# A scan layer, two FFNs and a higher-order linear attention in one kernel: front rounds, one q product, weight parts and a bias put in other places of a hand-written order

## The chip, the cores and the metric

The kernel runs as one program on one core of a Trainium2 chip. The metric is the device time of one execution in microseconds (us), as the median of several runs. One profiled execution beside them gives the trace from which all durations here are read.

## The reference

The input x has the shape (2, 2048, 256) in f32. Four layers are added to it one after the other, each on a layer norm of x:

```python
x = x + scan_layer(_layernorm(x))
x = x + ffn(_layernorm(x))
x = x + hla(_layernorm(x))
x = x + ffn(_layernorm(x))          # the same weights

# scan_layer: RMS norm with gamma, then
qkva = einsum('bnd,ed->bne', xn, w_qkva); q, kv, a = three parts; a = sigmoid(a)
s_t = a_t * s_(t-1) + kv_t;  out = q * s

# ffn: ternary weights w_t = clip(round(w / mean|w|), -1, 1)
out = gelu(x @ W1.T + b1) @ W2.T + b2                 # 256 -> 1024 -> 256

# hla: 16 heads of 64 dims; per head and time step
kC = k @ C;  G += k (x) kC;  S += k (x) k;  C += q (x) v
out = q @ (S @ C - G)                                 # then all heads @ W_o
```

## The kernel before, in words

x (4096 rows) stays in SBUF as `x_sb`, 32 chunks of 128 rows; a *block* is 4 chunks (512 rows, 8 blocks), a *pair* is the n-th chunk of both batches (16 pairs). The program has three stages in time: the front (0 to 227 us), attention (227 to 940 us, the last FFN's first two blocks woven into its end) and the rest of the last FFN. The order of the instructions on PE, DVE, ACT and POOL is the order in which the Python code issues them (`manual_schedule`); every engine works through its own list and waits, with semaphores, for what the others have to deliver, or for a buffer to come free. SP's queue carries most of the transfers.

**Front** (`front`, L563 to L746). The scan layer runs ahead of the FFN. The loop over `i` makes one *round* per block: `ffn_in` (L505) gives the 1024 hidden columns in 8 steps of 4 products (L512; PE) with a Gelu each (L518; ACT), and after two of them ACT casts the pair to a high part (L491) and DVE subtracts it for the low part (L497). `ffn_out` (L523) makes 4 x 16 output products with both parts (L536) and DVE adds them to x. The FFN's products run in fp32r, each operand x or h as hi plus lo, so the normed rows are cast and subtracted too, transposed. What a block needs ahead of its round is cut into steps: `fs_` (statistics on DVE L162 and L163, four small POOL operations L173 to L181), `fq_` (rows on ACT L194, then the squares of the transpose through DRAM: DVE, two kinds of SP transfers), and `fe_` (`halves_end`: the hi cast on ACT L202, the lo subtraction on DVE L203). `ffn_bias` (L550) adds b2 to a block: a copy of one column of `b2_sb` onto itself on DVE (L552), which ties the order, then 1024 columns on POOL (L554). Rounds 4 to 7 have no scan work; they take the later blocks' steps, the attention's first norm (the three functions in `then`: `attention_stats`, `attention_rows`, `attention_turned`) and, on POOL, the weight parts in `later`.

**Weight parts.** q, k and v of one pair are each made by seven products in place of eight (`class Seven`, Strassen-Winograd). They need sums of quarters of the weights: `weights_kv` (L465) makes four of 128x512 for each of wk, wv and wq with POOL instructions L469 to L472 (T3 overwrites a quarter of the weight itself). `pair_sums` (L768) makes the sums of the pair's rows (POOL L778, four of 128x128). wv is loaded ahead of the rounds, wq in round 5.

**Attention** (`attention`, L756 to L1216). 32 steps s = (n, b): pair n, batch b. A step computes the 64x64 head products (`products`, `inter`, `intra`: L887, L904, L918), the state updates (`update`), and the product with W_o (`outward`, L967). The matrices k and u are needed in two layouts; the transpose (*turn*) goes DVE L259 (32x32 squares), SP to DRAM and back, ACT L986. Between them stand the `Seven.go` calls of the next pair. `go(i)` makes product i and then its copy from PSUM on ACT (i = 1, 5, 6, 4; L847 to L864) or its addition on DVE (0, 7, 3; L838). PSUM is divided by tag: oT and uT each have two banks, ps four; a product into a bank waits until the last content is out. The loop's prologue (from L1008) makes pair 0's seven products of k, q and v, and the statistics, rows and turn of pair 1. In the last pairs `last` (class `Last`) does the same for the first block of the last FFN: its `part` method issues one transfer pair of a weight that comes back from DRAM (`weights(True)`: w1r over wk; `weights(False)`: w2r over wv), on ACT's queue. `last.begin` sets up the first block's `ffn_in`, and `fill(n)` runs n of its 8 steps between the steps of the last pair. Then the loop at L1370 does the last FFN over the 8 blocks: `ffn_out` of block i, `ffn_bias` of block i + 1.

A product may be split by columns: `in_two` and `first_in_two` list the products of k and v that are made as two of 256 columns in place of one of 512; the second list holds for pair 0 only.

The instructions themselves come to the engines by DMA: the page's queue "instruction" has 158 packets in 2.59 MB.

Of the kernel before, what the change touches and what calls it, by code (L numbers as in the profile page):

```python
# [23 lines left out]
P = 128  # L24
B, T, D = 2, 2048, 256
ND = D // P
# [18 lines left out]
def kernel(  # L45
# [456 lines left out]

        return Hidden(g0, room), lambda a: pool.tile([P, 2, BT], FP, tag="h", bufs=2, name=f"h{g0}_{a}")

    def ffn_in(g0, rhs, hid, stage_, tag="ps"):  # L505


        for f in range(NF):
            ph = bank([P, BT], f"h{g0}_{f}", tag)
            for d in range(ND):  # L510
                for k, r in enumerate(rhs):
                    nc.tensor.matmul(  # L512
                        ph, lhsT=w1r[:, d, f * P : (f + 1) * P], rhs=r[:, d, :],
                        start=(d == 0 and k == 0), stop=(d == ND - 1 and k == 1),
                    )
            if f % 2 == 0:
                h = stage_(f // 2)
            nc.scalar.activation(h[:, f % 2, :], ph, AF.Gelu, bias=b1_sb[:, f : f + 1])  # L518
            if f % 2 == 1:
                hid.split(h)  # L520
            yield
# [34 lines left out]
    def run(steps, n=None):  # L556
        for _ in steps if n is None else zip(range(n), steps):
            pass
# [4 lines left out]
    def front(scan_pool, ffn_pool, tern_pool, then, later):  # L563
# [112 lines left out]
        for i in range(NB):  # L676
            u, g0 = i + 5, blocks[i]
            more, scans = i + 1 < NB, u < len(units)
            hid, staged = hidden(ffn_pool, g0)
            steps = ffn_in(g0, fn.pop(i), hid, staged)  # L680
            if i == 0:
                ffn_bias(g0)
            if scans:
                ys[u] = []
                products = scan_steps(scan_pool, units[u][0], xnT[u], last[units[u][0] // CPB], ys[u], 2 if i > 0 else 1)
                for j in range(4):
                    run(products, 1)
                    run(steps, 1)
                    if i == 0 and j == 0:
                        a_(4)  # L690
                        fq_(1)
                run(products)
                if i == 3:
                    fq_(5, scan_pool, "xn")
            else:
                run(steps, 4)
                if i == 4:
                    fs_(7)
                if i == NB - 2:
                    then[0]()  # L700
            if u + 1 < len(units):
                s_(u + 1)
            if i == 0:
                fs_(2)
            run(steps)
            if u + 1 < len(units):
                r_(u + 1)
            if i == 5:
                wq = const.tile([P, ND, H * DK], FP, tag="wq", name="wq")
                nc.sync.dma_start(out=wq, in_=w_q.rearrange("(c p) e -> p c e", p=P))  # L710
            if not more:
                wo = const.tile([P, NPR, D], FP, tag="wo", name="wo")
                nc.sync.dma_start(out=wo, in_=w_o.rearrange("(c p) e -> p c e", p=P))
                then[2]()

            steps = ffn_out(g0, hid, tag="out")
            if i > 3 and i - 4 < len(later):
                later[i - 4]()
            if i == 2:
                ffn_weights_away()  # L720
            if scans:
                fe_(i + 1)
                ffn_bias(blocks[i + 1])
                run(steps, 2)
                a_(u)
                run(steps, 3)
                if u + 1 < len(units):
                    t_(u + 1)
            if i < 3:
                fq_(i + 2)  # L730
                fs_(i + 3)
                if i == 2:
                    fs_(6)
            elif i == 3:
                fq_(6)
                fe_(5)
            elif i + 2 < NB:
                fe_(i + 2)
                ffn_bias(blocks[i + 1])
                if i + 3 < NB:  # L740
                    fq_(i + 3)
            elif more:
                ffn_bias(blocks[i + 1])
            if i == NB - 2:
                then[1]()
            run(steps)  # L746


# [7 lines left out]
    def attention(keep, pool, state, last):  # L756
# [22 lines left out]
            pairs[n] = x, S  # L779

        in_two = {"kN": (1, 5, 3), "vN": (1, 5)}
        first_in_two = {"kN": (2, 4, 6, 7), "vN": (2, 4, 6)}

        class Seven:

# [29 lines left out]
            def product(self, at, i, tag=None):  # L815

                new = tag is not None
                shape = [P, NPR // 2, P] if self.nm == "qT" else [P, HK]
                if new:
                    setattr(self, at, bank(shape, f"h{self.nm}{self.n}_{at}", tag))  # L820
                to = getattr(self, at)
                if self.nm == "qT":
                    for j in range(NPR // 2):
                        nc.tensor.matmul(  # L824
                            to[:, j, :], lhsT=self.B[i][:, j * P : (j + 1) * P], rhs=self.A[i],
                            start=(new and j == 0), stop=True, skip_group_check=True,
                        )
                else:
                    m = 2 if i in in_two[self.nm] or self.n == 0 and i in first_in_two[self.nm] else 1
                    for j in range(m):  # L830
                        cols = slice(j * HK // m, (j + 1) * HK // m)
                        nc.tensor.matmul(  # L832
                            to[:, cols], lhsT=self.A[i], rhs=self.B[i][:, cols],
                            start=(new and j == 0), stop=True, skip_group_check=True,
                        )
# [170 lines left out]

        NS = len(steps)
        pair_sums(0)  # L1008
        stats = norm_stats(norm_pool, pair(1), bias=True)
        k, q, v = Seven(0, "kN", "oT"), Seven(0, "qT", "uT"), Seven(0, "vN", "oT")  # L1010
        k.go(2, 1, 0, 5)
# [21 lines left out]
        for s in range(NS):  # L1033
# [24 lines left out]
                k.go(2)  # L1058
            if first and s > 0:
                units_end(s - 1)  # L1060
            if s < NS - 2:
                last.part()
            elif s == NS - 2:
                last.part()
            if s >= 3:
                outward(s - 3, 1)
# [5 lines left out]
            if not more and not first:  # L1072
                units_end(s - 1)
            evict(s, "uT")
            if not more:
                if first:
                    units_out(s)
# [61 lines left out]
            if not more:  # L1139
                fill(1)  # L1140
                if first:
                    turn_end(s + 1, "kT")
                else:
                    last.his()
                    last.second_rows()
            elif first:
                k.go(*((6, 3, 7) if s > 0 else (3,)))
            else:
                v.go(7)
                q.go(7)  # L1150
                if s == NS - 3:
                    last.part()
                v.go(3, 4)
                q.go(3)
            last.part()
            if first and s > 0 and more:
                units_out(s)
# [5 lines left out]
            if not more:  # L1163
                if first:
                    fill(1)
                    last.his()
                last.los()
            elif first:
                k.go(4)
                if n + 2 < CPB:  # L1170
                    xn = norm_rows(norm_pool, pair(n + 2), stats)
                else:
                    last.rows()
            else:
                q.go(4)
            if not first and s + 2 < NS:
                keys_out(s + 2)
# [7 lines left out]
                last.turned()  # L1185
            if s == NS - 4:
                last.weights(True)
            last.part()
            if s == NS - 3:
                last.part(None)  # L1190
                last.weights(False)
# [22 lines left out]
        outward(NS - 1, 0)  # L1214
        outward(NS - 1, 1)
        last.halves(2)  # L1216

    pairs = {}

# [15 lines left out]
    class Last:  # L1235
# [69 lines left out]
        def begin(self, first):  # L1305
            if first:
                self.hid = Hidden(self.g0, self.halves_room)
                self.hid.held = []
                self.steps = ffn_in(self.g0, self.rhs, self.hid, self.staged)

        def fill(self, n):
            run(self.steps, n)
# [25 lines left out]
    with (  # L1338
        tc.tile_pool(name="scan", bufs=2) as scan_pool,
        tc.tile_pool(name="ffn1", bufs=2) as ffn_pool,  # L1340
        tc.tile_pool(name="tern", bufs=2) as tern_pool,
        tc.manual_schedule(engines=by_hand),
    ):

        warm = bank([P, P], "warm")
        for _ in range(12):
            nc.tensor.matmul(warm, lhsT=ones, rhs=ones, start=True, stop=True)
        nc.scalar.activation(table, ones[:, :1], AF.Sigmoid)
        front(
            scan_pool, ffn_pool, tern_pool, (attention_stats, attention_rows, attention_turned),  # L1350
            [lambda: weights_kv(wk, wk_t), lambda: weights_kv(wv, wv_t), lambda: weights_kv(wq, wq_t)],
        )
    front_ctx.close()

# [1 line left out]
    with tc.tile_pool(name="keep", bufs=3) as keep_pool:  # L1356
# [10 lines left out]
        with tc.tile_pool(name="ffn2", bufs=1) as ffn_pool, tc.manual_schedule(engines=by_hand):  # L1367
            two_rings()
            steps, rhs, raws = last.outs, last.turns, {}
            for i, g0 in enumerate(blocks):  # L1370
                more, ahead = i + 1 < len(blocks), i + 3 < len(blocks)
                if i > 0:
# [6 lines left out]
                    steps = ffn_out(g0, hid, True, "out")  # L1379
                    if i + 2 < len(blocks):  # L1380
                        rhs[i + 2] = halves_end(raws.pop(i + 2), rows_room(ffn_pool, blocks[i + 2], bufs=2))
                if more:
                    ffn_bias(blocks[i + 1])
                if ahead:
                    if i > 0:
# [40 lines left out]
```

## Time and profile before

| what | us |
|---|---|
| three runs: lowest, median, highest | 1054.04, 1056.1, 1056.45 |
| the profiled execution: its own time | 1052.7 |
| its span in the trace | 1050.9 |
| front: PE's first product of attention starts at | 227.09 |
| granted TensorE clock, mean over the span | 1.0 |

The page divides the span in 40 slices of 26.3 us; a digit is the busy share in tenths:

```
PE   9999999999999999999999999999999999999998
POOL 3433233831101001010010110101101001023430
PEclk9999999999999999999999999999999999999999
```

PE is busy in every slice, at full clock. POOL is used in the front, then little until the last FFN's biases. The share alone says nothing of a moment in which PE waits: those are found in the timeline, as the distance between the start of a group of products and the start of the next, against the usual distance. A line of the timeline reads: start in us, length in us (from the first to the last of a run of equal instructions), engine, line of the code, operation, out<-in, shape, count; a bracket at its end gives the idle time of the engine just before and what ended it. "issue" in a bracket is time in which no semaphore held the engine.

### The profile page before, as it was taken

Reading aid. Unit: us, or ns where it says so; the run is one execution under the profiler, and the core shown is the slowest. Engines: PE = TensorE matmul, PEld = TensorE weight load, DVE = VectorE, ACT = ScalarE, POOL = GpSimd, SP = SyncE. Lnnn points to the kernel's source line nnn. Section 1 sums busy time; section 2 is a strip of 40 time slices with the busy share of each in tenths; the row PEclk is TensorE's granted clock in tenths of the full one; section 3 lists DMA queues with packets and bytes.
Section 4 is the critical chain, followed back from the end, with each engine's and each line's share of the span. In section 5 each row is a group of like instructions: output and inputs, shape, how many; then the busy total and the mean of one; then the engine's idle time right before and its main releaser. Section 6 shows DMA issues by size and latency. Waiting matters only on the chain.

```text
span 1050.9 us, 43998 instructions
## 1 busy us (share of the span) xinstructions
PE 1042.0 (99%) x20166; PEld 851.0 (81%) x20166; DVE 724.7 (69%) x1063; ACT 612.7 (58%) x813; POOL 187.8 (18%) x282
## 2 busy tenths in 40 slices
PE   9999999999999999999999999999999999999998
PEld 7568889897777877788878787788877878889888
DVE  7987678846675765757656666666676666668863
ACT  4567779755645555455554455545555455659874
POOL 3433233831101001010010110101101001023430
PEclk9999999999999999999999999999999999999999
DMA  9231112203432423424324233242332435123321
GB/s 315 81 120 41 41 41 81 81 21 123 143 119 88 141 95 116 137 75 137 111 97 143 84 131 125 75 143 101 124 120 79 134 124 153 54 82 120 121 82 41
DMA packets 80828, 111.26 MB, mean 106 GB/s; under 512 B 8321, under 2 KB 66561, under 8 KB 80385
## 3 DMA queue, kind: packets, MB, share of 16 engines
q1 hardware_dynamic: 79024, 106.07, 30.6%
q8 instruction: 158, 2.59, 1.1%
q10 hardware_dynamic: 1584, 2.36, 0.8%
q14 instruction: 30, 0.24, 0.1%
q0 software_dynamic: 32, 0.00, 0.0%
HBM read 57.81 MB, written 50.59 MB: 103 GB/s over the span
## 4 chain that ended last, share of the span: by engine, by line
PE 84%; DVE 1%; ACT 1%; POOL 0%; issue 0%; ACTq 0%; POOLq 0%
PE hy L967 11%; PE o L536 9%; PE h L512 9%; PE hkN_X L832 6%; PE hp L887 6%; PE hqT_X L824 6%; PE hvN_X L832 6%; PE hoT L904 3%; PE huT L918 3%; PE hS L944 3%; PE huT L904 3%; PE hoT L918 3%; PE hM L944 3%; PE hqT_Z L824 3%; PE hkN_Z L832 3%; PE hvN_Z L832 3%
## 5 line engine op out<-in xcount | busy, mean ns | idle before, releaser
L893 DVE TENSOR_TENSOR p<-hp,mask 128x512 f32<-128x512 f32 x128 | 82.1, 683 | 82.7 <-PE hp L887 82.7
L967 PE MATMUL hy<-wo,oT 128*128 128x256 f32 x512 | 124.0, 386 | 0.0
L967 PEld LDWEIGHTS hy<-wo,oT 128*128 128x128 f32 x512 | 93.5, 190 | 18.9 <-issue 6.7
L778 POOL TENSOR_TENSOR S<-xnT 128x128 f32<-128x128 f32 x30 | 13.9, 462 | 511.2 <-ACT xnT L312 511.2
L497 DVE TENSOR_TENSOR hl<-h,hh 128x1024 fp32r<-128x1024 f32 x60 | 78.5, 1312 | 32.2 <-ACT hh L491 31.9
L518 ACT ACTIVATE h<-h,b_sb 128x512 f32<-128x512 f32 x120 | 77.7, 684 | 38.5 <-PE h L512 36.5
L929 ACT COPY uT<-huT 128x512 f32<-128x512 f32 x32 | 18.8, 586 | 126.6 <-PE huT L918 126.6
L194 ACT ACTIVATE xn<-x_sb,nb,rs 128x256 f32<-128x256 f32 x124 | 65.2, 593 | 23.4 <-POOL nb L180 23.4
L956 DVE TENSOR_TENSOR S<-S,hS 128x512 f32<-128x512 f32 x60 | 41.2, 687 | 42.0 <-PE hS L944 39.0
L259 DVE STREAM_TRANSPOSE squN<-uT 128x1024 f32<-128x1024 f32 x31 | 63.7, 2056 | 4.6 <-ACT uT L931 4.2
L259 DVE STREAM_TRANSPOSE sqkT<-kN 128x1024 f32<-128x1024 f32 x32 | 65.9, 2059 | 1.3 <-ACT kN L864 1.3
L986 ACT COPY kT<-rawkT 128x1024 f32<-128x1024 f32 x32 | 66.7, 2083 | 0.0
L986 ACT COPY uN<-rawuN 128x1024 f32<-128x1024 f32 x31 | 64.5, 2080 | 0.7 <-ACT xh_last L202 0.3
L491 ACT CAST hh<-h 128x1024 fp32r<-128x1024 f32 x60 | 63.1, 1051 | 1.9
L536 PE MATMUL o<-w2r,hl 128*128 128x256 f32 x256 | 61.1, 281 | 0.2
L536 PE MATMUL o<-w2r,hh 128*128 128x256 f32 x256 | 61.2, 281 | 0.0
L554 POOL TENSOR_TENSOR x_sb<-x_sb,b_sb 128x1024 f32<-128x1024 f32 x16 | 39.8, 2486 | 119.4 <-DVE b_sb L552 77.4
L536 PE MATMUL o<-w2r_back,hh 128*128 128x256 f32 x248 | 60.2, 284 | 0.0
L536 PE MATMUL o<-w2r_back,hl 128*128 128x256 f32 x248 | 60.0, 281 | 0.0
L864 ACT COPY vN<-hvN_X 128x512 f32<-128x512 f32 x16 | 9.4, 587 | 78.8 <-PE hvN_X L832 78.8
L162 DVE BATCH_NORM_STATS2 st<-x_sb 128x6 f32<-128x256 f32 x128 | 51.1, 400 | 2.4 <-DMA x_sb<-in_x_dram 2.4
L838 DVE TENSOR_TENSOR kN<-kN,hkN_Y 128x512 f32<-128x512 f32 x16 | 11.0, 685 | 57.0 <-ACT kN L847 57.0
(228 smaller groups left out, 2591.9 us busy)
## 6 DMA issues: line engine op xcount, KB each, us to landing
dsqkT<-sqkT SPq DMA_DIRECT2D x32, 512.0 KB, 3.5
rawkT<-dsqkT SPq DMA_DIRECT2D x128, 128.0 KB, 3.5
dsquN<-squN SPq DMA_DIRECT2D x31, 512.0 KB, 3.3
rawuN<-dsquN SPq DMA_DIRECT2D x124, 128.0 KB, 3.0
dsqxn<-sqxn SPq DMA_DIRECT2D x14, 512.0 KB, 2.7
rawxn<-dsqxn SPq DMA_DIRECT2D x56, 128.0 KB, 3.0
out_dram<-x_sb SPq DMA_DIRECT2D x15, 256.0 KB, 2.9
x_sb<-in_x_dram SPq DMA_DIRECT2D x7, 512.0 KB, 9.0
```

The lines of the kernel that those rows point to most:

```text
L194: nc.scalar.activation(xn[:, c, :], x_sb[:, g, :], AF.Identity, bias=nb[:, c : c + 1], scale=rs[:, c : c + 1],)
L259: nc.vector.transpose(to, src)
L491: nc.scalar.copy(hi, h)
L497: nc.vector.tensor_tensor(self.lo[a], h, self.hi[a], ALU.subtract)
L512: nc.tensor.matmul(ph, lhsT=w1r[:, d, f * P : (f + 1) * P], rhs=r[:, d, :], start=(d == 0 and k == 0), stop=(d == ND - 1 and k == 1),)
L518: nc.scalar.activation(h[:, f % 2, :], ph, AF.Gelu, bias=b1_sb[:, f : f + 1])
L536: nc.tensor.matmul(to, lhsT=h[f // 2][:, f % 2, c * P : (c + 1) * P], rhs=w2r[:, f, :], start=(f == 0 and k == 0 and (c % 2 == 0 or at == ...
L824: nc.tensor.matmul(to[:, j, :], lhsT=self.B[i][:, j * P : (j + 1) * P], rhs=self.A[i], start=(new and j == 0), stop=True, skip_group_check ...
L832: nc.tensor.matmul(to[:, cols], lhsT=self.A[i], rhs=self.B[i][:, cols], start=(new and j == 0), stop=True, skip_group_check=True,)
L893: nc.vector.tensor_tensor(d[s][nm][:, h], banks[h], mask8, ALU.mult)
L967: nc.tensor.matmul(py, lhsT=d[s]["oT"][:, p, :], rhs=wo[:, p, :], start=(p == 0), stop=(p == NPR - 1),)
L986: act(t, d[s]["r" + nm].rearrange("p t q -> p q t"))
```

## The change

- **Front, steps in other rounds.** `fe_(5)` goes from the end of round 3 to the output products of round 4, with `fe_(6)` behind it; `fs_(7)` from round 4 to the start of round 5; `fq_(7)` from round 4 to round 5, behind wq's load on SP; `fe_(7)` from round 5 to round 6. The first attention pair's statistics (`then[0]`) go from the hidden products of round 6 to its end, its rows and turn (`then[1]`) from the end of round 6 into round 7, behind two of its eight hidden steps.
- **Weight parts.** wk's go from round 4 to the end of round 6; wv's and wq's from rounds 5 and 6 to attention's prologue, behind `pair_sums(0)` and ahead of pair 1's norm on POOL.
- **One q product.** At s = 1, `q.go(4)` moves from behind `turn_end` (ACT), `inter` and `products` to right behind `q.go(3)`; at other odd s it stays.
- **w1r's return.** At s = NS-4, NS-3 and NS-2, calls of `last.part()` go; one stands behind `evict` at s = NS-3, so each transfer is issued about one turn later.
- **Second block's bias in the last FFN.** `ffn_bias(blocks[1])` goes from the loop at the end (i = 0) to the end of `attention()`, behind `last.halves(2)`.
- **Splits in two.** At the last pair (n = CPB-1) v's products 2, 3, 4, 6, 7 are made in two halves of 256 columns; so are the products of the first two steps of `ffn_in` at `last.begin`.

```diff
-    def ffn_in(g0, rhs, hid, stage_, tag="ps"):
+    def ffn_in(g0, rhs, hid, stage_, tag="ps", in_two=0):
...
-                    nc.tensor.matmul(
-                        ph, lhsT=w1r[:, d, f * P : (f + 1) * P], rhs=r[:, d, :],
...
+                    m = 2 if f < in_two else 1
+                    for j in range(m):
+                        t = slice(j * BT // m, (j + 1) * BT // m)
+                        nc.tensor.matmul(
+                            ph[:, t], lhsT=w1r[:, d, f * P : (f + 1) * P], rhs=r[:, d, t],
...
             else:
+                if i == 5:
+                    fs_(7)
+                elif not more:
+                    run(steps, 2)
+                    then[1]()
                 run(steps, 4)
-                if i == 4:
-                    fs_(7)
-                if i == NB - 2:
-                    then[0]()
...
             steps = ffn_out(g0, hid, tag="out")
-            if i > 3 and i - 4 < len(later):
-                later[i - 4]()
...
+            if i == 4:
+                fe_(5)
...
             elif i == 3:
                 fq_(6)
-                fe_(5)
-            elif i + 2 < NB:
-                fe_(i + 2)
+            elif i == 4:
+                fe_(6)
                 ffn_bias(blocks[i + 1])
-                if i + 3 < NB:
-                    fq_(i + 3)
-            elif more:
+            elif i == 5:
                 ffn_bias(blocks[i + 1])
-            if i == NB - 2:
-                then[1]()
+                fq_(7)
+            elif i == 6:
+                fe_(7)
+                ffn_bias(blocks[i + 1])
+                then[0]()
+                later()
             run(steps)
...
-        first_in_two = {"kN": (2, 4, 6, 7), "vN": (2, 4, 6)}
+        ends_in_two = {"kN": {0: (2, 4, 6, 7)}, "vN": {0: (2, 4, 6), CPB - 1: (2, 3, 4, 6, 7)}}
...
         pair_sums(0)
+        weights_kv(wq, wq_t)
+        weights_kv(wv, wv_t)
         stats = norm_stats(norm_pool, pair(1), bias=True)
...
-            if s < NS - 2:
-                last.part()
-            elif s == NS - 2:
+            if s == NS - 2:
                 last.part()
...
             evict(s, "uT")
+            if s == NS - 3:
+                last.part()
...
                 q.go(3)
+                if s == 1:
+                    q.go(4)
             last.part()
...
-            else:
+            elif s > 1:
                 q.go(4)
...
             if s == NS - 4:
                 last.weights(True)
-            last.part()
             if s == NS - 3:
                 last.part(None)
...
         last.halves(2)
+        ffn_bias(blocks[1])
...
-                self.steps = ffn_in(self.g0, self.rhs, self.hid, self.staged)
+                self.steps = ffn_in(self.g0, self.rhs, self.hid, self.staged, in_two=2)
...
-            [lambda: weights_kv(wk, wk_t), lambda: weights_kv(wv, wv_t), lambda: weights_kv(wq, wq_t)],
+            lambda: weights_kv(wk, wk_t),
...
-                if more:
+                if more and i > 0:
                     ffn_bias(blocks[i + 1])
```

## Prediction, before the run

> **What bounds the kernel now.** I read the page first, then the chain of waits, then the timelines of the engines around each edited place.
>
> ```profile
> PE 1042.0 (99%) x20166; PEld 851.0 (81%) x20166; DVE 724.7 (69%) x1063; ACT 612.7 (58%) x813; POOL 187.8 (18%) x282
> ```
>
> PE is busy 99% of the span, so no other engine's work counts by itself. The change hardly alters PE's work; it can only remove or make moments in which PE waits. The chain in order of time gives the length of the front's late rounds as the distance between the starts of their first products (columns: start, length, what):
>
> ```profile
> 166.32 7.46 PE h L512 x32
> ...
> 181.53 1.88 PE h L512 x8
> ...
> 197.35 7.46 PE h L512 x32
> ...
> 212.28 7.50 PE h L512 x32
> ```
>
> Round 6 takes 212.28-197.35 = 14.93 us, round 4 takes 15.21, round 5 takes 15.82. So rounds 4 and 5 lose 0.28 and 0.89 us. The timelines say why for round 5: DVE's three subtractions of L497 (1.22 us each elsewhere) took 7.06 us while POOL was in L470 to L472 and L554.
>
> **Front (rounds 4 to 7).** The hi/lo split of block 5 leaves round 3 for round 4, and wk's parts leave round 4, wv's round 5, wq's round 6. With no POOL work beside DVE's subtractions I take back the whole 1.17 us of rounds 4 and 5. The work that hides the moved split: a Gelu sequence ends 10.4 us after its round's start (round 7: 222.71-212.28), so ACT casts block 5 from 176.7 (2.36 us), DVE subtracts (2.21 us) until 181.3, and round 5's second matmul needs it at 181.25+0.23 = 181.5. The cover is 0.2 us, as for block 7 at the end of round 6; were it gone, a late split is paid one for one. In round 7 the rows of the first attention pair now stand between the first and second Gelu pair. They wait for POOL, which first does the bias of block 7 (2.4 us, behind DVE's split at about 211.1), then the four small norm operations: 1.62 us alone (229.29 to 230.91), 3.26 beside DVE's subtractions (206.15 to 209.41). So the rows start at 215.3 to 216.3 instead of 214.8, take 1.09, and three Gelu pairs of 2.25 us follow; the output products, one quarter each 1.87 us from 218.6, then wait 0.3 to 1.3 us for the last subtractions. I take 0.9. Front: -1.17+0.9 = -0.3 us (ends -1.2 and +0.3).
>
> **Start of attention.** wq's and wv's parts are moved behind the first pair's sums on POOL, ahead of the second pair's norm. POOL's timeline (start, length, operation):
>
> ```profile
> 209.37 1.29 POOL L469 TENSOR_TENSOR wq_t<-wq 128x512 f32<-128x512 f32 x1
> ...
> 214.49 2.40 POOL L554 TENSOR_TENSOR x_sb<-x_sb,b_sb 128x1024 f32<-128x1024 f32 x1
> 227.39 0.46 POOL L778 TENSOR_TENSOR S<-xnT_first 128x128 f32<-128x128 f32 x1 [10.50 <-PE o L536]
> ...
> 229.29 0.22 POOL L174 TENSOR_SCALAR rs<-mv 128x2 f32<-128x2 f32 x1
> ```
>
> Four parts take 214.49-209.37 = 5.12 us. The sums cannot start before the front's last product ("<-PE o"), so wq's and wv's eight parts run from 229.29 to 239.5, and the norm of pair 1 (1.62 us) ends at 241.15 instead of 230.91. Who waits for it, and what is queued behind, ACT's timeline and PE's show:
>
> ```profile
> 236.52 1.09 ACT L194 ACTIVATE xn<-x_sb,nb,rs 128x256 f32<-128x256 f32 x2
> 237.97 0.59 ACT L864 COPY kN<-hkN_X 128x512 f32<-128x512 f32 x1 [0.36 <-PE hkN_X L832]
> ```
>
> ```profile
> 238.66 1.08 PE L832 MATMUL hvN_X<-wv,xnT_first 128*128 128x256 f32 x4
> ```
>
> ACT runs in order: the rows of pair 1, then the copy of kN, and v's first product reuses the bank that this copy empties (238.56 done, 238.66 product). Now: rows from 241.2, copy from 242.2 to 242.8, product at 242.9. PE stands 4.24 us. POOL's parts themselves are in time (wq's first at 230.6 against its use at 234.05; wv's first at 235.7 against 240.47). DVE's next transpose hangs on the same copy and shifts with it. The stall could be longer where a POOL part meets a DVE subtraction of two SBUF operands (2.16 us instead of 1.29 at 192.02), but DVE here adds from PSUM and transposes, beside which L472 at 185.07 and L471 at 183.80 took 1.29 and 1.31. I take 4.24 (ends 4.2 and 6).
>
> The stall has a price of its own, the clock. At the end of the program, the windows view (PE busy and granted clock of a stretch):
>
> ```profile
> 1045.00:1050.00 5.00, 2.41 (x21) 2.20 (x19) 1.44 (x3) 0.00 (x0) 0.00 (x0) 1.00 0.32 107
> 1050.10:1050.90 0.80, 0.00 (x0) 0.00 (x0) 0.00 (x0) 0.00 (x0) 0.00 (x0) 0.50 0.00 0
> ```
>
> PE's last matmul ended at 1045+2.41 = 1047.4 and by 1050.1 the clock was 0.50: 2.7 us without work were enough once. No gap in the kernel now exceeds 0.83 us. At the start the 24 warm-up records took 5.09 us (212 ns each against 111 at 234.05), so half clock lasts some 4.5 us (1.05 to the first full-clock record at 5.58). If the clock falls 2.7 us into the gap of 4.1 and rises 4.5 us later, 3.1 us of work run at half speed and lose 1.55. I take 1.5 (ends 0 and 2.3, half of 4.5). The Trainium skill ("TensorE: Matmul & The Clock Gate", Part 1: the HAM clock gate) speaks against the change too: one idle window of about 3.4 us sends the array to half clock and one busy window brings it back. It would make of this, an estimate, 0 or up to 1.7 us by phase; this case's 2.7 us is shorter than that page's window, so the row is what I go by.
>
> **One q product ahead of two turns (s=1).** Now:
>
> ```profile
> 280.12 1.16 PE L904 MATMUL huT<-qT,S 64*64 64x64 f32 x64 [0.68 <-ACT qT L864]
> ...
> 283.20 1.51 PE L918 MATMUL huT<-p,kN 64*64 64x64 f32 x61
> ```
>
> The 0.68 goes, as qT's copy then runs before kT's turn. But the first products on the way come 0.9 us later (279.17 instead of 278.28 for p2's end), and DVE does p2 (1.29), then a transpose (started 279.61, 2.09), then p1, which PE's 283.20 step waits for: 279.3 + 1.2 + 2.0 = 282.5, p1 done 283.8 instead of 283.55. The wait moves three steps on and ends 0.34 us later than now. I take +0.34 (ends -0.84 and +0.4).
>
> **The tail.** w1r's parts come back later (one turn on), and block 1's bias goes to the end:
>
> ```profile
> 862.12 0.57 PE L918 MATMUL huT<-p,kN 64*64 64x64 f32 x23
> 863.52 0.81 PE L918 MATMUL huT<-p,kN 64*64 64x64 f32 x41 [0.83 <-issue]
> ```
>
> ```profile
> 888.09 0.15 DVE L552 COPY b_sb<-b_sb 128x1 f32<-128x1 f32 x1 [2.54 <-POOL x_sb L554]
> ```
>
> The first stall is "issue": no semaphore held PE. The trace's packets on the instruction queue (158 of 16 KB) come every 256 instructions; this one started 2.8 us after PE entered the block before, while w1r's two parts (issued 856.56) and a transpose's rows filled the queues, against 0.5 to 0.9 us elsewhere. Without them the step takes 0.98 instead of 2.03: -1.05 (ends -1.05 and 0). The parts' new places, 866 to 873, lie beside slow 128-wide products; they land 18 us before h needs them at 891.5. The skill ("Runtime: NRT & Kernel Launch", Instruction fetch mechanics) holds the crossing of such a block to be mostly hidden. By that the move gains nothing and the sum would be 1.05 higher; the 0.83 us above differ from it.
>
> The second pair: DVE's b_sb copy of block 1 waits for POOL to finish block 0's bias, and p1 behind it comes 2 us late; PE loses 0.25 at 888.65 and 0.48 inside the step: -0.73 (ends -0.73 and 0). At its new place the bias (2.85 us on POOL) has the next block's products, 15 us, to hide in.
>
> **Splits in two.** 128x512 products cost 0.861 us, split ones 0.865; five of them +0.03. The h products: 233 ns whole, 2 x 117 split: 0. They add 36 PE instructions (20 and 16, with weight loads), which move the block borders behind 870. Two more stalls there (0.35 at 896.8, 1.0 at 898.7, the second "issue") could go or return elsewhere; I take 0 (ends -1.4 and +1.1).
>
> **Sum.** -0.3 + 4.24 + 1.5 + 0.34 - 1.05 - 0.73 + 0.03 = +4.0 us. The profiled execution took 1052.7 (span 1050.9), so 1056.7 for such a one; the runs' median is 1056.1, so I predict 1060.1.
>
> **Rivals.** (1) The clock stays full through the gap: +2.5, 1058.6, not slower by what can be told. For it: the 2.7 us is one reading, at a program's end. It decides where the gap falls under what the monitor looks at. 27%. (2) The shifted block borders starve another burst of 64x64 steps, or round 7 costs its upper end: +1.0 to +1.5 on the forecast, 1061.4. The steady turns have little room (0.5 to 1 us), but borders there are unchanged. 14%. (3) Both stalls at 897 to 899 go and the clock stays full: +1.1, 1057.2. 9%. (4) POOL gets to the parts early, so the change doesn't do what its order says: without 4.24 and 1.5 the sum is -1.7, with the two stalls -3.1, 1053. The sums' wait for the front's last product speaks against it. 4%.
>
> **Numbers.** The forecast has 46%, with its own range 1058.8 to 1061.8. The range 1056.6 to 1062.6 leaves out rival 4, half of rival 3 and the upper part of rival 2. About 3.2 us (0.3%) is what can be told from no change. Slower: most of the forecast (0.40), rival 2 (0.13), a little of rival 1 (0.04): 0.57. Faster: 0.04. Same: the rest, 0.39.
>
> **What would show it.** Right: POOL L469 to L472 of wq and wv behind L778 at the front's end; ACT's L194 waiting for POOL nb there; PE idle some 4 us ahead of hvN_X, followed by slow records; rounds 4 and 5 at 14.9; no "issue" stall in the huT step of turn 28. Wrong: a short gap at hvN_X, a full clock behind it, or a new loss in rounds 4 to 7.

## The result, and the profile after

The changed kernel takes 1061.36 us in the median of six runs (1058.36 to 1061.86), the kernel before 1054.78 beside it (1052.25 to 1056.45): a ratio of 1.0058, 95% interval 1.0041 to 1.0076, slower by 6.6 us. The span of the profiled execution grows by 8.1 us, from 1050.9 to 1059.0; the profiled execution of before lies 2.1 us under its median, that of after (1060.79) 0.6 us, so 1.5 of the 8.1 us are no part of the difference of the medians.

Where the 8.1 us come in is read by setting the starts of the same products of both traces side by side; a step in their difference is time gained or lost there:

| place (time in after) | forecast | measured |
|---|---|---|
| rounds 4 and 5 (up to 196) | -1.17 | -1.17 |
| round 7 (211 to 227) | +0.9 | +1.26 |
| gap ahead of hvN_X (239 to 243) | +4.24 | +3.96 |
| half clock behind it (243 to 259) | +1.5 | +1.84 |
| q's product 4 at s = 1 (280 to 291) | +0.34 | +0.12 |
| w1r's parts off the fetch (868) | -1.05 | -1.05 |
| block 1's bias, p at 891 | -0.73 | -0.82 |
| v's splits (by themselves) | +0.03 | +0.03 |
| new issue stall at 895 | 0 | +2.15 |
| a second half clock (898 to 902) | 0 | +1.51 |
| old stalls at 897 and 899 gone | 0 | -1.27 |
| last FFN, output products (960, 1006) | 0 | +1.40 |
| start-up (6) and small drifts | 0 | +0.17 |
| sum | +4.0 | +8.13 |

The start of attention, PE, ACT and POOL in the timeline of after (start, length, engine, line, operation):

```profile
238.01 1.05 PE L830 MATMUL hqT_X<-S,wq 128*128 128x128 f32 x8
242.85 1.89 PE L838 MATMUL hvN_X<-wv,xnT_first 128*128 128x256 f32 x4 [3.78 <-ACT kN L870]
```

```profile
241.24 1.09 ACT L194 ACTIVATE xn<-x_sb,nb,rs 128x256 f32<-128x256 f32 x2 [4.40 <-POOL nb L180]
242.23 0.56 ACT L870 COPY kN<-hkN_X 128x512 f32<-128x512 f32 x1
```

```profile
229.38 1.27 POOL L469 TENSOR_TENSOR wq_t<-wq 128x512 f32<-128x512 f32 x1
...
238.23 1.27 POOL L472 TENSOR_TENSOR wv_t<-wv,wv_t 128x512 f32<-128x512 f32 x1
...
240.97 0.23 POOL L180 TENSOR_SCALAR nb<-nb 128x2 f32<-128x2 f32 x1
```

Read backwards, each line waits for the next: product for copy, copy behind rows, rows for the norm, norm behind eight parts. The product's four matmuls take 1.89 us in place of 1.08: the clock. The windows view of after (PE, PEld, DVE, ACT and POOL busy, then the granted clock) in stretches of 3.41 us, first around this gap, then around 895:

```profile
239.66:243.07 3.41, 0.22 (x1) 0.23 (x2) 0.24 (x1) 1.56 (x3) 1.29 (x4) 1.00 0.59 154
243.07:246.48 3.41, 3.41 (x13) 3.06 (x13) 2.31 (x2) 0.59 (x1) 0.00 (x0) 0.50 0.23 94
246.48:249.89 3.41, 3.41 (x79) 3.07 (x79) 1.77 (x3) 1.17 (x2) 0.00 (x0) 1.00 0.50 151
...
895.02:898.43 3.41, 1.46 (x64) 1.33 (x59) 1.98 (x3) 1.72 (x3) 1.71 (x4) 1.00 0.58 142
898.43:901.84 3.41, 3.41 (x31) 3.19 (x33) 0.45 (x1) 1.04 (x2) 0.00 (x0) 0.50 0.83 246
```

Idle time of PE in a stretch is its length less PE's busy time: 3.41 less 0.22 is 3.19 us, 3.41 less 1.46 is 1.95 us. Each of these two stretches is followed by one at half clock.

Round 7 (ACT in after): the rows wait 1.39 us for POOL, which does block 7's bias first, and all Gelu pairs behind them come later. In PE's timeline this is the wait of 0.58 us at 221.30 for DVE's third subtraction, itself 1.57 us long in place of 1.23 beside POOL's parts of wk:

```profile
216.31 1.09 ACT L194 ACTIVATE xn<-x_sb,nb,rs 128x256 f32<-128x256 f32 x2 [1.39 <-POOL nb L180]
```

```profile
221.30 0.39 PE L540 MATMUL o<-w2r,hl 128*128 128x256 f32 x1 [0.58 <-DVE hl L497]
```

The tail, PE in after: the huT step at 868, which lost 1.05 us to "issue" before, runs through, as does the one at 894 that waited for p. The loss comes one step later. (w1r's four transfers are issued at 869.57, 874.15, 877.67 and 878.03, before at 856.56, 856.93, 869.02 and 872.52. Less the 5 us by which after is late here, the first two moved by 8 and 12 us, the third by 3.5, the last hardly.)

```profile
868.30 1.16 PE L924 MATMUL huT<-p,kN 64*64 64x64 f32 x64
...
893.80 1.16 PE L924 MATMUL huT<-p,kN 64*64 64x64 f32 x64
894.78 0.30 PE L924 MATMUL hoT<-p,vN 64*64 64x64 f32 x8
897.03 1.04 PE L924 MATMUL hoT<-p,vN 64*64 64x64 f32 x56 [1.95 <-issue]
```

In the trace's packets of the instruction queue, PE enters a block of 256 instructions at 890.6 and the packet for the next one starts at 894.74, 4.1 us later; most others start 0.6 to 1.2 us after such a border. Ahead of it stand three transfers of w2r (256 KB each, issued from 888.24 to 889.27 on ACT's queue) and the squares of kT (512 KB, issued 889.57 on SP's). And in the last FFN, ACT waits for transposed rows that it had in time before (there the cast of xh_last followed the rows' instruction at once):

```profile
946.15 2.26 ACT L202 CAST xh_last<-rawxn 128x1024 fp32r<-128x1024 f32 x1 [0.74 <-DMA rawxn<-dsqxn]
```

### The profile page after: what moved, and what is told of

Read it like the earlier page. It is cut to its first block, busy times and chain, and to the rows that moved or that the text cites. A ratio compares the mean times of both kernels' runs of the same rounds, so it can differ in the third digit from the quotient of the medians.

```text
span 1059.0 us, 44037 instructions
## 1 busy us (share of the span) xinstructions
PE 1044.1 (99%) x20184; PEld 855.3 (81%) x20184; DVE 718.7 (68%) x1063; ACT 612.4 (58%) x813; POOL 182.4 (17%) x282
## 4 chain that ended last, share of the span: by engine, by line
PE 77%; ACT 3%; POOL 3%; DVE 2%; issue 2%; ACTq 0%; POOLq 0%; DVEq 0%
PE hy L973 11%; PE o L540 6%; PE h L515 6%; PE hvN_X L838 6%; PE hp L893 6%; PE hkN_X L838 5%; PE hqT_X L830 5%; PE hoT L910 3%; PE hS L950 3%; PE huT L924 3%; PE huT L910 3%; PE hM L950 3%; PE hoT L924 3%; PE hqT_Z L830 3%; PE hvN_Z L838 3%; PE hkN_Z L838 2%
## 5 line engine op out<-in xcount | busy, mean ns | idle before, releaser
L497 DVE TENSOR_TENSOR hl<-h,hh 128x1024 fp32r<-128x1024 f32 x60 | 73.8, 1232 | 38.5 <-ACT hh L491 38.2
L259 DVE STREAM_TRANSPOSE sqxn<-xn 128x512 f32<-128x512 f32 (+1 forms) x35 | 46.6, 1368 | 6.1 <-ACT xn L194 6.1
```

Of the source, the lines that this page charges most:

```text
L259: nc.vector.transpose(to, src)
L497: nc.vector.tensor_tensor(self.lo[a], h, self.hi[a], ALU.subtract)
```

## The experiments

Times are medians beside the runs of the kernel before on the same chip; "a single run" is one time and its profile. Offsets are read from the traces as in the table above.

**1. Pair 1's norm ahead of the parts.**

```diff
         pair_sums(0)
+        stats = norm_stats(norm_pool, pair(1), bias=True)
         weights_kv(wq, wq_t)
         weights_kv(wv, wv_t)
-        stats = norm_stats(norm_pool, pair(1), bias=True)
```

> The changed kernel with one thing undone in effect: the four small norm operations of pair 1 go ahead of wq's and wv's eight parts on POOL. Theory (the parts delay the norm, so the rows, so kN's copy, so v's first product): the wait of 3.78 us ahead of hvN_X and the 3.4 us of half clock behind it both go, and wq's and wv's parts are still in time; 3.96 + 1.71 us less than 1061.4, so 1055.7 (1054.5 to 1056.5). Rival 1 (the parts are then late themselves, PE waits for wq_t or wv_t instead): a wait of 1 us or more at hqT_Z or hvN_Z, 1057 or more. Rival 2 (the gap is an effect of something else, such as the product's bank): the gap stays, 1061.

Measured: 1054.01 us against 1055.06 (ratio 0.9996, 0.9985 to 1.0006), the same as before. The gap is gone in PE's timeline, and the clock behind it is full:

```profile
237.84 1.05 PE L830 MATMUL hqT_X<-S,wq 128*128 128x128 f32 x8
238.73 1.08 PE L838 MATMUL hvN_X<-wv,xnT_first 128*128 128x256 f32 x4
```

So with the order of two things on POOL turned round, the norm's 1.6 us and the parts' 10, the loss of the medians is gone. The two medians differ by 7.35 us, the two terms of the table account for 5.8; the rest is not placed. Part of it can be the clock in the tail: the profile here still has a half clock there, from 891.70, behind an issue stall of 2.11 us, but seven of the ten runs show a mean clock of 1.000, where the changed kernel's six show 0.995 to 0.998. Neither rival holds.

**2. Six parts, then the norm, then two.** wv's last two parts stand behind the norm.

> The changed kernel with pair 1's norm behind six of the eight parts (two of wv's come after it). Six parts end at about 237.0, the norm at 238.6, rows and copy at 240.3: the wait at hvN_X should be 1.4 us. Theory (the clock falls only where most of a 3.4 us window is idle): no half clock there, and the wait costs just its length: 1061.4 - 2.55 - 1.71 = 1057.1. Rival (any wait above the 0.83 us that the kernel before had is enough): a half clock record of 3.4 us behind it, 1058.8.

Measured: 1055.43 us against 1055.06. The wait is 1.33 us, and the step after it runs at full clock:

```profile
240.44 1.13 PE L836 MATMUL hvN_X<-wv,xnT_first 128*128 128x256 f32 x4 [1.33 <-ACT kN L868]
```

```profile
237.07:240.48 3.41, 2.08 (x14) 1.77 (x13) 0.61 (x2) 1.56 (x3) 3.08 (x7) 1.00 0.40 163
240.48:243.90 3.42, 3.42 (x23) 3.14 (x24) 3.42 (x4) 1.12 (x2) 0.78 (x1) 1.00 0.71 214
```

1.34 us idle of 3.41 leave the clock alone. The median is 1.42 us above that of experiment 1, about the length of the wait. The time is 1.7 us under the forecast; the second half clock, at the tail, was not there either: the issue stall of 1.71 us there left 1.39 us idle in one stretch, and the rest fell into the next.

**3. The parts' move alone.** The kernel before with wv's and wq's parts in the prologue and nothing else.

> The kernel before with one part of the change: wv's and wq's parts move from rounds 5 and 6 to the start of attention, behind the sums and ahead of pair 1's norm; nothing else. Theory: +3.96 (wait at hvN_X) + 1.7 (half clock) - 0.9 (round 5's subtractions no longer beside POOL) = +4.8 us, 1059.5. Rival (the loss comes from the parts together with the other moves of the front): less than +3 us.

Measured: 1060.58 us against 1055.06 (1.0064, 1.0041 to 1.0087), +5.5. The move alone brings most of the change's loss. What all its other parts bring, gains and losses together, is the remaining 1 us, which lies within the interval here (4.3 to 9.2 us). Here the clock stayed low for two stretches:

```profile
237.49:240.90 3.41, 0.75 (x7) 0.56 (x5) 0.00 (x0) 0.48 (x1) 2.56 (x5) 1.00 0.50 157
240.90:244.31 3.41, 2.28 (x6) 1.93 (x7) 2.30 (x2) 1.25 (x4) 0.00 (x0) 0.50 0.25 52
244.31:247.73 3.42, 3.42 (x14) 3.06 (x13) 1.55 (x3) 0.59 (x2) 0.00 (x0) 0.50 0.38 156
```

The gap spans both first stretches: the second still had 1.13 us idle, and the third stayed at half.

**4. The rows of the first pair earlier.** At the end of round 6, `then[0]()` stands ahead of `ffn_bias`.

> The changed kernel with round 6's end in another order: the first attention pair's statistics and norm ahead of block 7's bias on DVE and POOL. Theory (round 7 lost 1.27 us because the rows waited for POOL, busy with the bias, and delayed three Gelu pairs; 0.35 of it because POOL's wk parts ran beside DVE's subtractions): the rows start at about 214.9 in place of 216.3, the wait of 0.58 us at the output products' hl goes to nearly nothing, front's end 0.9 us earlier. Rival (the subtractions beside POOL alone are the cause): no change at the front's end, since the bias then runs beside them too.

Measured (a single run): 1057.71 us. The front ends 0.95 us earlier (1.06, less 0.11 of the start), the rows start at 214.69, and the wait of 0.58 us at the output products is gone. DVE's four subtractions run even longer now beside POOL's bias and wk's parts (2.78, 1.36, 1.79 and 1.79 us); three of them start early enough that PE does not feel it. The fourth ends at 224.32, and the product that needs it starts at 224.38, some 0.3 us late. So of the 1.26 us that round 7 lost, the rows' place behind the bias made 0.95, and the subtractions beside POOL's work make the 0.3 that are left.

**5. Block 1's bias back.** `ffn_bias(blocks[1])` stands in the loop at the end again.

> The changed kernel with block 1's bias of the last FFN back in the loop at the end, so that DVE's b_sb copy waits for POOL ahead of p at 893 again. Theory (the instruction fetch at 895 is late on its own account, whenever p comes): p is 2 us later and PE waits 0.8 us there, but the issue stall behind it shrinks by as much, and the hidden products start as before (within 0.2 us). Rival 1 (the bias' place decides when the fetch is served): the issue stall at 895 goes, hidden products 1.3 us earlier. Rival 2 (both add up): 0.8 us later.

Measured (a single run): 1058.25 us. PE waits for p again (0.17 and 0.27 us idle at 892 and 893, 0.73 lost), and the issue stall behind it is 1.38 us in place of 1.95; measured from the products at 860, the hidden products start 0.26 us later. That is nearer to the theory than to either rival: the bias' 0.82 us are gained only if the next block of instructions is there. The profile shows one more thing. The gap at hvN_X was 3.78 us again, but no half clock followed:

```profile
237.62:241.03 3.41, 1.45 (x11) 1.20 (x9) 0.00 (x0) 0.00 (x0) 3.08 (x6) 1.00 0.51 185
241.03:244.45 3.42, 1.60 (x10) 1.50 (x11) 1.62 (x1) 1.99 (x4) 0.17 (x1) 1.00 0.43 105
244.45:247.86 3.41, 3.41 (x81) 3.06 (x81) 2.24 (x5) 1.33 (x3) 0.00 (x0) 1.00 0.37 154
```

The gap fell across a border of these stretches, 1.97 and 1.81 us idle on either side. In experiment 6 the same gap (3.80 us) was cut into 1.83 and 1.97 us, and there half clock did follow. Of the eight profiles with the whole gap (after and experiments 3 to 9) this is the only one without half clock behind it.

**6. v's last products whole.** `ends_in_two` without its entry for the last pair.

> The changed kernel with v's products 2, 3, 4, 6, 7 of the last pair whole again (20 PE instructions fewer, so that the borders of the 256-instruction blocks behind 870 us fall 20 instructions later, where they were in the kernel before). Theory (the border is what met the traffic of w2r's return and kT's rows): the 1.95 us of issue at 895 goes, and with it the second half clock record at 898 (1.5 us); the stalls of the kernel before at 897 and 899 (0.35 and 1.0 us) come back in part: 1057.7 to 1059. Rival (the moved transfers of w1r starve the fetch, wherever the border is): an issue stall of 1.5 us or more stays at the same place, 1061.

Measured: 1059.24 us against 1055.06 (1.0045, 1.0023 to 1.0068), 4.2 us over the kernel before where the changed kernel had 6.6; the two intervals overlap, so the profile has to carry the reading. The issue stall stayed (1.91 us at 897, and a second of 0.92 at 902), so the theory fails there: the border's place by v's 20 instructions is not what makes the fetch late. What went is the last FFN's loss (no wait at xh_last, no wait at the output products, 1.4 us), and the half clock behind the stall: the 1.91 us fell across a border of two stretches, with 0.95 and 0.96 us idle in them.

**7. w1r's parts where they were.**

> The changed kernel with w1r's transfers issued where the kernel before issues them. Theory (the new places of w1r's parts delay the fetch at 891): the fetch behind the border at 890.6 comes 2.4 us after it as before in place of 4.1, so the 1.95 us stall and the half clock behind it go (-3.6), while the stall at 868 comes back (+1.05 to +1.5): 1058.8. Rival (w2r's three transfers right behind each other, which both kernels have, are enough): the stall at 895 stays, the one at 868 is added: 1062.5.

Measured: 1061.85 us against 1053.51 (1.0076, 1.0053 to 1.0099). The stall at 868 is back ("issue" 1.08 us idle, 1.30 lost), as in all four profiles with the old places and in none of the ten with the new ones. The fetch behind 890 comes after 2.4 us, and two smaller stalls (0.51 and 1.40) stand for the one of 2.15. Experiment 4, with w1r's new places, shows the same two (0.55 and 1.39); so w1r's places do not decide this, and neither side of the expectation holds.

**8. w2r's first two transfers later.** `last.part(2)` at the end of step NS-3 goes.

> The changed kernel without the two w2r transfers issued together at the end of step NS-3; they follow one by one in step NS-2. Theory (768 KB of w2r on ACT's queue, issued within 1.1 us, stand in front of the instruction fetch): the fetch comes within 1.5 us of its border, the issue stall of 1.95 us at 895 goes and with it the half clock of 3.4 us: 1061.4 - 2.16 - 1.5 = 1057.7, or 1058.7 if another stall of up to 1 us comes where the later transfers go. Rival (the turn's squares and the rows on SP's queue delay it): the stall stays.

Measured: 1058.95 us against 1053.51 (1.005, 1.0031 to 1.0068), 5.4 us over the kernel before where the changed kernel had 6.6, again with overlapping intervals. The step at 894 runs through, then a new stall comes behind the transfers' new place:

```profile
894.59 1.11 PE L924 MATMUL hoT<-p,vN 64*64 64x64 f32 x64
895.63 0.50 PE L515 MATMUL h<-xh_last,w1r_back 128*128 128x256 f32 x2
...
902.25 0.45 PE L893 MATMUL hp<-qT,uT 64*64 64x64 f32 x16
904.19 0.52 PE L893 MATMUL hp<-qT,uT 64*64 64x64 f32 x21 [1.49 <-issue]
```

The fetch that came 4.1 us late now comes after 1.8; the next but one, behind w2r's third transfer (issued 898.54) and the squares of uN (898.75), after 3.4. The squares of kT still stand ahead of the first of these fetches (issued 889.38, in after 889.57); what no longer stands there are w2r's two transfers, and with them went most of its delay. In the new stall one transfer and the squares of uN meet; which of the two counts there is not separated. Over all profiles: in the twelve in which w2r's three transfers stand together ahead of this fetch, its packet starts 2.3 to 4.3 us after the border; in this one, with one transfer ahead, 1.8, and in the two of experiments 11 and 12, also with one, 1.2. The eight split hidden steps, at full clock here, take 2.07 us (895.63 to 897.70), as whole ones do before (891.51 to 893.58).

**9. The hidden products whole.** `ffn_in` at `last.begin` without `in_two`.

> The changed kernel with the first two hidden steps of the last FFN whole again (16 PE instructions fewer behind 900 us; v's products stay split). In every run of the changed kernel's kind with both splits, xh_last at 946 waited 0.74 to 1.07 us for rows that land while an instruction block (16 KB) is fetched, and PE waited 0.72 us at 959; with v whole this wait is not there. Theory (36 more instructions bring that fetch some 2 us earlier, onto the rows' transfer): with 20 more it comes after them, no wait at xh_last, none at the output products of block 1, the end 1.0 to 1.4 us earlier. Rival (v's split itself, or the bias' place, delays the rows): the 0.7 us wait stays. The hidden products themselves take as long split as whole at full clock.

Measured (a single run): 1058.48 us. xh_last no longer waits (cast at 943.98 right behind the rows) and block 1's output products run through, 0.87 us gained there; the smaller wait at 1003 (0.40) stays. The issue stall is 1.13 us here, with a second of 0.74 at 901, and no half clock follows.

**10. Both splits alone on the kernel before.**

> The kernel before with one part of the change: both splits in two, 36 PE instructions more. Theory (the splits cost by where the borders of the instruction blocks fall, not by their own length): +0.03 us by themselves; the wait of about 0.7 us at xh_last and at block 1's output products appears, as in the changed kernel: +1.0 to +1.4 at the end; the stall at 862 unchanged. Whether an issue stall of about 2 us at 890 comes with them is open: yes if the borders decide it, no if it needs the new places of w1r's parts or of the bias.

Measured (a single run): 1052.59 us against 1053.66. The theory fails: no wait at xh_last, and the end is 0.07 us earlier. Nor is there an issue stall at 890; the one at 864 is 0.52 us longer than in the kernel before, and the one at 899 is gone. The splits by themselves cost nothing in sum; with either one undone the changed kernel's loss at xh_last is gone too, so it needs both splits and other moves, which points to a meeting in time of two transfers. The traces speak for the instruction fetch, with one exception. The last of the four transfers of these rows takes 3.93 to 4.27 us in the seven profiles in which xh_last waits, and in each a packet of the instruction queue starts 1.3 to 2.1 us after it is issued (in after, issued 942.12, packet 943.46). In six of the seven profiles without the wait it takes 2.86 to 2.94 us, and no packet starts before 2.6 us. The seventh is this run: a packet after 1.88 us, and yet 2.99 us. So a packet within the transfer goes with the wait, but is not enough for it.

**11. A version put together from the runs.** Experiments 1, 4 and 6 in one, and w2r's four transfers spread: two in step NS-2, two in NS-1.

```diff
                 last.weights(False)
-                last.part(2)
...
-            last.part()
+            if s != NS - 2:
+                last.part()
```

(The second edit stands at two places: ahead of the updates, and behind the last products of the step.)

> What the runs point to, put together: the changed kernel with pair 1's norm ahead of wq's and wv's parts, the first pair's norm ahead of block 7's bias, v's last products whole, and w2r's four transfers spread (two in step NS-2, two in step NS-1). Theory: 3.96 + 1.7 (gap and clock), 0.95 (round 7), about 1.4 (rows of the last FFN) and 2 (fetch at 895) less than 1061.4: 1051.4 (1050 to 1053), under the kernel before by some 3 us. Rival (the fetch's stalls only move, as they did with w2r later): 1053 to 1055, no different from before.

Measured: 1049.56 us against 1053.66: ratio 0.9958, 0.9943 to 0.9973, 0.4% faster than the kernel before, and under the changed one. The clock is full from 5.7 us to the end, and the tail has no issue stall at 868, 895 or 899; one with 0.26 us idle is left at 914. Its first lines of the page:

```profile
span 1047.8 us, 44019 instructions
...
PE 1040.6 (99%) x20174; PEld 851.0 (81%) x20174; DVE 720.2 (69%) x1063; ACT 612.1 (58%) x813; POOL 182.6 (17%) x282
```

**12. The same with q's product 4 back.**

> The kernel put together from the runs, with q's product 4 of step s = 1 back behind the turn of kT, as in the kernel before. Theory (the move costs a little, since the wait at 280 only goes to p1 three steps later): PE waits some 0.6 us ahead of huT<-qT,S for qT's copy again, the wait of 0.77 us ahead of huT<-p,kN at 280.8 goes, and the stretch from there to the next pair's first product is 0.1 us (0.34 by the prediction) shorter; no difference that the times can show from 1049.6. Rival (the move gains the 0.68 us that it was charged with in the chain): 0.3 us or more longer.

Measured: 1049.57 us against 1054.09 (0.9955, 0.9938 to 0.9972). In PE's timeline the wait for qT is back (0.68 us idle at 279.32), the one for p at 283 shrinks, and the next pair's first product comes 0.12 us earlier. The move costs 0.12 us, as in the table.

## Why the prediction was right, and where not

- **Forecast and time.** 1060.1 us were forecast, 1061.36 came, inside the forecast's own range of 1058.8 to 1061.8. That it is so near is in part luck. The forecast set +4.0 us on a median of three runs, 1056.1; beside the changed kernel the kernel before took 1054.78, so the difference to be forecast was 6.6 us, and 1.3 of the missing 2.6 were hidden by the base. The kernel before is not always at full clock, as its profile is: of the twenty runs beside experiment 1, nine show a mean clock of 0.998 and take 1055.37 to 1056.01 us, the others 0.999 or 1.000 and 1051.91 to 1055.12. What the forecast rests on is right: the slowdown comes from the gap at hvN_X and the half clock behind it, and these are shown: taking POOL's order back removes both (experiment 1), the move alone makes them (3), and a shorter gap costs its length alone (2).
- **The gap.** 3.96 us against 4.24. From PE's first product of attention (227.30) to hvN_X (242.85) 15.55 us went by, by the forecast 15.81 (227.09 to 242.9). The four sums took 1.78 us of it in place of 1.90, the eight parts 10.21 in place of 10.24; the rest is some hundredths at the copy and the product.
- **The clock.** Half clock lasted 3.41 us, not 4.5, and cost 1.84 (1.71 at once). The step that took "2.7 us without work" as the time to the fall was wrong in kind: it falls at the end of a stretch, so the gap's place against the stretches decides, as rival 1 held (experiment 5 is its case). That the term came out near its 1.5 is in part luck of that place. By the Trainium skill ("TensorE: Matmul & The Clock Gate", Part 1: the HAM clock gate) one idle window of about 3.4 us is needed. The window's length agrees with the 3.41 us here; an idle one was not needed, 1.95 us in it were enough.
- **Front.** Rounds 4 and 5 to the hundredth; round 7 lost 1.26 in place of 0.9, near the upper end of that term. The rows' wait for POOL was right (0.95 by experiment 4). Not counted were wk's parts on POOL beside the subtractions of round 7, two of which took 1.57 and 1.56 us in place of 1.23; some 0.3 us come from there.
- **s = 1.** The wait moved three steps on, as forecast; it cost 0.12, not 0.34. The prediction's own times for it, 283.8 against 283.55, give 0.25.
- **The tail** is where the sum is off. The gains at 868 and 891 were right (-1.87 against -1.78). The step that failed is "two more stalls there could go or return elsewhere; I take 0 (ends -1.4 and +1.1)": the old ones went (-1.27) and a new one of 2.15 us came, +0.88, inside those ends. But 2.15 us is long enough for a second half clock (+1.51), and the rows' transfer of the last FFN lost 1.40; neither was thought of. Rival 2 was right in kind (another burst starved, and round 7's upper end), though the splits' shifted borders, its cause, did not hold (6 and 10).
- **Left open.** Why the same fetch comes after 2.4 us in some executions and after 4.1 in others, with equal code. It is behind w2r's transfers (8); what else decides it was not found. So the tail's new losses (the stall, the half clock, the rows' transfer) are seen in the traces, but what brings them at these places is open in part.

## What to carry to other kernels

A helper engine's list is a queue: work moved "to where there is time" is paid in what stands behind it there, so put small operations that others wait for ahead of long ones that are needed late. Where PE is busy 99% of the span, look at transfers of a megabyte near bursts of short matmuls: there the next block of instructions can be what is late. Moving such a burst of transfers moved the stall here (8); in the kernel with the burst spread, among other edits, most of it was gone (11).

## What the runs showed of the hardware

- The clock is set in stretches of 3.41 us on a fixed grid: between the changes of the clock lie multiples of it (in after 238.93 = 70 of 3.413, 651.95 = 191), and half clock lasted one stretch, or two (6.83 in experiment 3). The grid's start against the program differs from run to run.
- By these profiles, PE's idle time within one stretch decides. In the 14 profiles, at full clock, 1.85 us and less never brought half clock behind it, 2.04 and more always did; between them 1.95 and 1.97 did, and another 1.97 did not. So one and the same gap of about 3.8 us cost 1.7 us more in one execution than in another.
- At half clock a stretch with 1.13 us idle did not bring full clock back; one without any did.
- Instruction blocks of PE came late behind other transfers: with w2r's three transfers of 256 KB and the squares of kT in front, the packet started 2.3 to 4.3 us after the border, where most others take 0.6 to 1.2, and bursts of 64x64 matmuls, in which 256 instructions last about 2 us by themselves, stood idle for up to 2.11 us (experiment 1).
